# Storing from ScalarE's queue what ScalarE has made, with the planner's ranks found anew

## The chip, the core and the metric

The kernel runs on one core of one Trainium2 chip. A core has five engines that run side by side, each with its own instruction stream that is worked off in order: TensorE (PE; its weight loads are shown as PEld), VectorE (DVE), ScalarE (ACT), GpSimd (POOL) and SyncE (SP). They wait for each other through semaphores. DMAs are started from the instruction stream of an engine: SyncE, ScalarE and GpSimd start them here. An instruction at the head of a stream that waits holds all that stand behind it.

The metric is the device time of one execution in microseconds (us). Before the change it is 1215.32 us, the median of three runs (1213.84 to 1217.02).

## What is computed

Two transformer layers on 4096 tokens (16 sequences of 256) of width 128, all in float32, each sublayer followed by a residual sum and a layer norm:

```
x = layernorm(x + attention0(x))    # RMS norm, 16 heads of 64, softmax over 256 keys, output projection, bias
x = layernorm(x + moe0(x))          # 8 experts of hidden 256, top 2, gelu, biases, and one shared expert
x = layernorm(x + attention1(x))    # 16 heads of 8; each token attends over its own 16 heads
x = layernorm(x + moe1(x))          # 8 experts of hidden 512, top 2, gelu
```

The experts' weights of one token are its two largest softmax probabilities, not normalised anew. The layer-1 attention works inside a token: its scores are a 16 x 16 matrix for every token.

## The kernel before

**Tiles.** The tokens are cut into eight groups (0 to 7) of 512, each held in SBUF as a tile of 128 partitions x 4 chunks x 128. Group 7 is special: its second half is not routed by lists but goes through all experts with resident weights (the "dense" way, function `dense`, tiles ph_d, po_d, h_d, wd).

**Stages.** Layer-0 attention runs through all groups as 128 units, one pair of heads and one sequence each (`attention0`): projections (pq, pk, pv), scores (s), row maximum on VectorE (nm), exp on ScalarE and scaling on GpSimd (pr), transposes (t, copied to pT), values (po, copied to oT), and the output projection (py). When the groups of a wave are through, its mixture of experts starts while attention goes on with later groups. There are five waves in layer 0 and three in layer 1. A wave goes through:

- routing (`route`): top 2 of 8, and the position of each (token, expert) row in a list that is sorted by expert and padded to tiles of 128 rows. One small product (pc) counts across partitions.
- sending (`send`, L904 and L905): GpSimd writes the tokens' rows to their positions in DRAM (rows) with indirect DMAs.
- the lists (`lists`): in blocks of up to four tiles, SyncE loads the rows (xq, L1014) and the expert's weights (wa, L1035 or L1039; wb, L1048; the expert's number is read into a register at L997). TensorE transposes the rows (px, copied to xqT), does the first product (ph, L1098), ScalarE the gelu (h, L1071 or L1077), TensorE the second product (po_e, L1118). Function `stored` copies po_e to a tile yq, on VectorE or ScalarE, and SyncE stores yq to DRAM (outs, L1136). There are 46 such stores. yq has three buffers.
- gathering (`gathered`, L934 and L948): GpSimd reads each token's two rows back from outs (y), and VectorE adds them with their gates.
- a layer norm (`normed`). In layer 0 the layer-1 attention follows (`attention1`, `chunk1`: pqkv, copied to qkv; then products and reduces qk_prod, sc, av_prod and o, mostly on VectorE and GpSimd). In layer 1, `last` norms into a tile ye (one buffer) and stores it to the output (L1431); the dense half does the same at the end of `sequence` (L1595). These are nine output stores.

`normed` scales either on VectorE (L399) or, with two more small GpSimd instructions, on ScalarE (L409). ScalarE has to load a table (ACT_TABLE_LOAD) whenever it goes from exp to gelu or back.

**What sets the order.** The order of every engine's stream is settled when the program is built, by a planner written into the kernel. Each piece of work is a strand (a Python generator). A strand says when it could go on and on which engine. The planner keeps an estimated clock per engine (`clk`), advances it by `work(engine, us, ...)`, and always takes the strand with the smallest start less a lead. Lead and rank come from the table `KEYS` (one pair of rank and lead for each kind of work), and from `PACE` for the sixteen halves of attention. Further constants steer choices: `COPY` (VectorE or ScalarE for a copy, in `copied`), `FAVOUR` (GpSimd or VectorE for a product), `SWITCH` and `SWITCH_BACK` (when to change ScalarE's table), and `SUMS` (from what lead of TensorE over VectorE the sums of the layer-1 attention go to TensorE, as the products o_sums, L1274). `moved` is the estimate of a DMA: the issuing engine's time, then a shared pipe. No instruction is moved after this.

Of the kernel before, what the change touches and what calls it, by code (L numbers as in the profile page):

```python
# [28 lines left out]
LAST = NG - 1  # L29
# [8 lines left out]
def two_layers(  # L38
# [98 lines left out]
    def cleared(layer, w):  # L137
# [13 lines left out]
        "copy qk": (-0.126, 0.098),  # L151
        "copy v": (0.258, 0.464),
        "copy p": (0.365, 0.67),
        "copy o": (-2, 0.171),
        "softmax": (-0.332, 0.347),
        "softmax 2": (-0.557, 0.071),
        "summed": (-1.741, 0.444),
        "normalised": (0.126, 0.737),
        "heads": (-0.897, 0.036),
        "w route": (0.203, 0.017),  # L160
        "w send": (-0.299, 0.32),
        "w shared": (-0.925, 0.219),
        "w loads": (-0.335, 0.546),
        "w turns 0": (-0.74, 0.23),
        "w turns 1": (-0.883, 0.07),
        "w firsts 0": (-0.387, 0.019),
        "w firsts 1": (1.618, 0.545),
        "w gelu": (-0.526, 0.095),
        "w seconds 0": (-0.551, 0.301),
        "w seconds 1": (1.137, -0.645),  # L170
        "w stored": (-1.046, -0.735),
        "w gathered 0": (0.929, 0.295),
        "w gathered 1": (0.397, -0.379),
        "w qkv": (-1.874, 0.602),
        "w attention1": (0.552, 0.037),
        "w attention1 2": (0.862, 0.362),
        "w sums": (0.545, 0.099),
        "w normed": (-0.751, 0.178),
        "d loads": (-1.222, 0.561),
        "d route": (0.341, 0.516),  # L180
        "d firsts": (-0.612, -0.163),
        "d gelu": (0.532, 0.418),
        "d seconds": (-0.409, -0.744),
        "d added": (-0.448, 0.337),
        "d normed": (-0.4, 1.013),
    }
    PACE = [-1.37, 1.462, -1.273, -1.636, 1.503, -0.385, -0.54, 1.281]
    PACE += [1.979, 0.872, 0.936, -0.178, 0.47, 1.169, 0.679, 1.086]
    now = [0]
    COPY = -0.06  # L190
    SUMS = 7.789
    FAVOUR = 0.378
    SWITCH, SWITCH_BACK = 0.582, 1.515
# [44 lines left out]
    def moved(size, *after, us=0.45, row=2048):  # L238

        at = max(work("SP", us, *after) + 0.1, pipe[0])  # L240
        pipe[0] = at + size / (270e3 if row >= 1024 else 200e3)
        return max(pipe[0], at + size / 150e3) + 1.6
# [6 lines left out]
    def closed(place, at):  # L249
        ends[place[0]][place[1]] = at  # L250
        return at
# [132 lines left out]
    def normed(y, o, tag, at):  # L384
# [12 lines left out]
        if max(clk["DVE"], at) + 1.9 <= max(clk["ACT"], at) + 1.4:  # L397
            for c in range(n):
                nc.vector.tensor_scalar(  # L399
                    o[:, c, :], y[:, c, :], mv[:, c, 0:1], r[:, c : c + 1], ALU.subtract, ALU.mult  # L400
                )
            return work("DVE", 0.05 + 0.35 * n, at, ports=True)
# [7 lines left out]
        return work("ACT", 0.35 * n, at)  # L410
# [558 lines left out]
    def lists(r):  # L969
# [159 lines left out]
        def stored(i, place, po, at):  # L1129
# [3 lines left out]
            y, k = Y.tile([P, QT, D], "yq")  # L1133
            at = closed(place, copied(y[:, 0:n, :], po[:, 0:n, :], at, free))
            yield at, "SP"
            nc.sync.dma_start(  # L1136
# [3 lines left out]
            Y.done[k] = r.stored[i] = moved(n * 65536, at, row=512)  # L1140
# [282 lines left out]
    def last(r, part):  # L1423
# [4 lines left out]
        at = yield from normed(tokens(part), y, "n1", at)  # L1428
        yield at, "SP"
        b = c0 // 2  # L1430
        nc.sync.dma_start(  # L1431
# [3 lines left out]
        return work("SP", 0.6, at)  # L1435
# [133 lines left out]
    def sequence(b=1):  # L1569
# [23 lines left out]
        at = yield from normed(x, y, "n1", at)  # L1593
        yield at, "SP"
        nc.sync.dma_start(out=grouped(out, LAST)[:, b], in_=y.rearrange("p c d -> p (c d)"))  # L1595
        held.remove("y1")
        work("SP", 0.6, at)
# [66 lines left out]
```

## Time and profile before

The profile is of one execution, which is not one of the three timed ones.

| quantity | value |
|---|---|
| median of the runs | 1215.32 us |
| profiled execution: its own time | 1245.39 us |
| profiled execution: span of its instructions | 1243.7 us |
| mean granted clock of TensorE in it | 0.943 of full |
| PE busy | 1109.0 us (89%) |
| DVE busy | 900.2 us (72%) |
| ACT busy | 706.0 us (57%) |
| POOL busy | 705.7 us (57%) |
| DMA moved | 132.47 MB, mean 107 GB/s |

The page has a row of digits for each engine: the span in 40 equal slices, each digit the busy share in tenths; PEclk is the clock that the throttle granted TensorE, also in tenths. The chain of waits follows the last instruction back, at each step to what released it, and gives start, length and what ran; "issue" is time in which an engine waited for nothing that the profile shows. Lists of waits give the engine and line, what it waited for, the total in us, the number of waits and the longest. SPq is SyncE's queue, which issues DMAs.

The rows of the stores, from the answers on the tiles yq and ye (duration least, median, most in ns; first and last start in us):

```profile
L1136 SPq DMA_DIRECT2D outs<-yq x46: 359/448/1400, 211.4 to 1211.8; - x46
L272 ACT COPY yq<-po_e x36: 478/585/672, 206.8 to 1205.3; 128x512 f32<-128x512 f32 x32, 128x384 f32<-128x384 f32 x4
L270 DVE COPY yq<-po_e x10: 548/686/693, 201.6 to 1211.2; 128x512 f32<-128x512 f32 x6, 128x384 f32<-128x384 f32 x4
L1431 SPq DMA_DIRECT2D out_dram<-ye x8: 345/383/1532, 1166.5 to 1240.5; - x8
```

### The profile page before, as it was taken

What the parts mean: (1) busy time and instruction counts of PE and PEld (TensorE: products, weight loads), DVE (VectorE), ACT (ScalarE), POOL (GpSimd) and SP (SyncE); (2) the same over time, 40 slices, a digit from 0 to 9 for tenths busy, and PEclk for the clock granted to TensorE, in tenths of its full rate; (3) what the DMA queues carried; (4) which work ended last, traced back from release to release, by engine and by line L of the source; (5) the groups of instructions that cost most, each with busy time, mean ns of one, the idle gap of its engine ahead of it and who ended that gap; (6) DMA issues with size and microseconds to landing.
All of it is one profiled execution on the core that took longest, in us unless ns stands there. A gap on an engine that the chain in (4) does not pass through costs nothing.

```text
span 1243.7 us, 22712 instructions
## 1 busy us (share of the span) xinstructions
PE 1109.0 (89%) x7336; PEld 814.5 (65%) x7336; DVE 900.2 (72%) x1811; ACT 706.0 (57%) x2050; POOL 705.7 (57%) x1089
## 2 busy tenths in 40 slices
PE   9999999979999999999998899987838896797883
PEld 5566667665665666766655677655738795697883
DVE  5767675478878888754877998888878795793433
ACT  5556566476665667676674687653544552342432
POOL 4434372557555468524769557767873546446666
PEclk9999999989999999999999999987888897798997
DMA  8900023430000021151003240135458874684952
GB/s 260 270 1 1 1 86 111 132 106 14 1 5 1 1 63 58 35 145 45 18 4 100 80 133 21 29 119 164 144 162 232 257 230 129 197 245 125 288 177 70
DMA packets 187208, 132.47 MB, mean 107 GB/s; under 512 B 12745, under 2 KB 171474, under 8 KB 187090
## 3 DMA queue, kind: packets, MB, share of 16 engines
q1 hardware_dynamic: 179410, 115.27, 31.6%
q0 software_dynamic: 7680, 15.74, 4.1%
q8 instruction: 59, 0.97, 0.3%
q14 instruction: 59, 0.48, 0.1%
HBM read 97.94 MB, written 33.03 MB: 105 GB/s over the span
## 4 chain that ended last, share of the span: by engine, by line
PE 66%; DVE 11%; POOL 8%; issue 6%; ACT 4%; DMA 2%; SPq 1%; ACTq 0%; DVEq 0%; POOLq 0%
PE s L574 9%; PE po L612 9%; PE t L591 9%; PE po_e L1118 6%; PE ph L1098 6%; POOL rows L905 5%; PE py L629 4%; PE pv L528 4%; PE pq L510 4%; PE pk L510 3%; DVE qk_prod L1216 2%; DMA xq<-rows 2%; PE po_d L1541 1%; POOL pr L558 1%; DVE sc L1220 1%
## 5 line engine op out<-in xcount | busy, mean ns | idle before, releaser
L558 POOL TENSOR_SCALAR pr<-pr,rs 128x256 f32<-128x256 f32 x512 | 253.0, 511 | 220.6 <-DVE rs L554 136.7
L543 ACT ACTIVATE pr<-s,nm 128x256 f32<-128x256 f32 x512 | 235.5, 474 | 26.1 <-DVE nm L537 23.0
L537 DVE TENSOR_REDUCE nm<-s 128x4 f32<-128x1024 f32 x128 | 156.1, 1220 | 58.0 <-PE s L574 53.2
L905 POOL DMA_INDIRECT rows<-x,r_pi x120 | 130.7, 1089 | 58.6 <-DVE r_pi L853 24.4
L934 POOL DMA_INDIRECT y<-outs,r_pi x120 | 120.0, 1000 | 65.8 <-issue 27.4
L612 PE MATMUL po<-pT,v 128*64 128x256 f32 x1024 | 146.0, 397 | 7.2 <-ACT h L1077 3.1
L1098 PE MATMUL ph<-xqT,wa 128*128 128x128 f32 x1028 | 132.8, 287 | 16.6 <-issue 14.2
L591 PE MATMUL t<-ident,pr 128*128 128x128 f32 x1024 | 144.4, 283 | 0.8 <-ACT h L1077 0.8
L591 PEld LDWEIGHTS t<-ident,pr 128*128 128x128 f32 x1024 | 115.7, 145 | 42.4 <-POOL pr L558 20.6
L1098 PEld LDWEIGHTS ph<-xqT,wa 128*128 128x128 f32 x1028 | 126.9, 202 | 22.6 <-issue 16.8
L270 DVE COPY pT<-t 128x512 f32<-128x512 f32 x163 | 106.8, 686 | 42.2 <-PE t L591 38.3
L574 PEld LDWEIGHTS s<-kT,qT 64*128 64x128 f32 x896 | 77.1, 186 | 84.2 <-issue 73.1
L574 PE MATMUL s<-kT,qT 64*128 64x256 f32 x896 | 127.0, 402 | 0.0
L1292 POOL TENSOR_TENSOR av_prod<-sc,qkv 128x1024 f32<-128x1024 f32 x35 | 89.9, 2577 | 50.7 <-ACT sc L1254 35.3
L272 ACT COPY oT<-po 128x256 f32<-128x256 f32 x99 | 36.9, 373 | 130.6 <-PE po L612 119.6
L612 PEld LDWEIGHTS po<-pT,v 128*64 128x64 f32 x1024 | 65.1, 137 | 67.6 <-issue 18.9
L543 ACT ACTIVATION_READ_ACCUMULATOR pr<-s,nm 128x1 f32 x512 | 105.5, 206 | 0.0
L1118 PE MATMUL po_e<-wb,h 128*128 128x128 f32 x648 | 84.3, 292 | 5.5 <-issue 5.5
L1118 PEld LDWEIGHTS po_e<-wb,h 128*128 128x128 f32 x648 | 82.6, 209 | 5.3 <-issue 4.8
L1216 DVE TENSOR_TENSOR qk_prod<-qkv 128x1024 f32<-128x1024 f32 x64 | 82.8, 1294 | 1.8 <-ACT qkv L272 1.8
L1267 DVE TENSOR_REDUCE o<-av_prod 128x64 f32<-128x1024 f32 x62 | 73.3, 1200 | 11.3 <-POOL apart L904 9.7
L1220 DVE TENSOR_REDUCE sc<-qk_prod 128x128 f32<-128x1024 f32 x64 | 78.1, 1220 | 2.2
(233 smaller groups left out, 1971.0 us busy)
## 6 DMA issues: line engine op xcount, KB each, us to landing
wa<-in_w_dram SPq DMA_DIRECT2D x190, 128.0 KB
wa<-in_w_dram SPq DMA_DIRECT2D x81, 256.0 KB
wb<-in_w_dram SPq DMA_DIRECT2D x81, 256.0 KB
xq<-rows SPq DMA_DIRECT2D x38, 256.0 KB
outs<-yq SPq DMA_DIRECT2D x38, 256.0 KB
rows<-clear SPq DMA_DIRECT2D x3, 1472.0 KB
rows<-clear SPq DMA_DIRECT2D x1, 2496.0 KB
rows<-clear SPq DMA_DIRECT2D x2, 1216.0 KB
```

The source lines that it names most:

```text
L270: nc.vector.tensor_copy(o, i)
L537: nc.vector.tensor_reduce(nm[u], s, AX.X, ALU.max, negate=True)
L543: nc.scalar.activation(pr[u][:, i, :], s[:, i, :], AF.Exp, bias=nm[u][:, i : i + 1], accum_out=su[u][:, i : i + 1],)
L558: nc.gpsimd.tensor_scalar(pr[u][:, i, :], pr[u][:, i, :], rs[:, i : i + 1], 1.0, ALU.mult, ALU.mult)
L574: nc.tensor.matmul(sc[u][:, j, qc, :], q[part, ts(qc, P)], k[part, :], start=True, stop=True,)
L591: nc.tensor.transpose(t[:, kc, ts(qc, P)], pr[u][:, 2 * j + qc, ts(kc, P)], ident)
L612: nc.tensor.matmul(po[j * DH : (j + 1) * DH, :], vs[g, p // 4, 2 * b + kc][:, ts(h, DH)], pT[u][j][:, kc, :], start=(kc == 0), stop=(kc == 1),
L905: i = nc.gpsimd.indirect_dma_start(out=rows[layer][w][:, :], out_offset=bass.IndirectOffsetOnAxis(ap=r.pos[:, k, c : c + 1], axis=0), in_= ...
L934: nc.gpsimd.indirect_dma_start(out=y, out_offset=None, in_=outs[layer][w][:, :], in_offset=bass.IndirectOffsetOnAxis(ap=r.pos[:, k, c0 + c ...
L1098: nc.tensor.matmul(ph[:, q - q0, c, :], was[i, q][0][:, c, :], xTs[i][0][:, q, :], start=True, stop=True)
L1118: nc.tensor.matmul(po[:, q, :], hs[i, q][0][:, c, :], wbs[i, q][0][:, c, :], start=(c == 0), stop=(c == nh - 1))
L1216: nc.vector.tensor_tensor(m, q3[:, ts(j, HALF)].unsqueeze(2).to_broadcast(full), k3.unsqueeze(1).to_broadcast(full), ALU.mult)
```

## The change

Two things are changed together.

First, a store goes out from the engine that made the tile. `normed` can now say which engine did the scaling (`who=True`). In `stored`, `last` and at the end of `sequence`, the DMA is issued by ScalarE if ScalarE wrote the tile, directly behind the copy or the scaling in ScalarE's own stream. If VectorE wrote it, the store stays with SyncE and its strand still has to be chosen by the planner for SyncE. `moved` charges the issue to that engine, and the estimate of a list store's issue is 0.55 us in place of 0.45.

Second, all constants of the planner but FAVOUR are new: the ranks and leads in KEYS, PACE, COPY, SUMS, SWITCH and SWITCH_BACK. The planner's rules are as before. With other constants the order of the instructions differs nearly everywhere on all engines, and so do some choices of engine.

```diff
     KEYS = {
-        "copy qk": (-0.126, 0.098),
-        "copy v": (0.258, 0.464),
-        "copy p": (0.365, 0.67),
+        "copy qk": (-0.686, 0.094),
+        "copy v": (0.244, 0.271),
+        "copy p": (-0.684, 0.892),
...
-    COPY = -0.06
-    SUMS = 7.789
+    COPY = -0.04
+    SUMS = 6.956
     FAVOUR = 0.378
-    SWITCH, SWITCH_BACK = 0.582, 1.515
+    SWITCH, SWITCH_BACK = 0.754, 1.251
...
-    def moved(size, *after, us=0.45, row=2048):
+    def moved(size, *after, us=0.45, row=2048, e="SP"):
 
-        at = max(work("SP", us, *after) + 0.1, pipe[0])
+        at = max(work(e, us, *after) + 0.1, pipe[0])
...
-    def normed(y, o, tag, at):
+    def normed(y, o, tag, at, who=False):
...
-            return work("DVE", 0.05 + 0.35 * n, at, ports=True)
+            at = work("DVE", 0.05 + 0.35 * n, at, ports=True)
+            return (at, "DVE") if who else at
...
-        return work("ACT", 0.35 * n, at)
+        at = work("ACT", 0.35 * n, at)
+        return (at, "ACT") if who else at
...
+            was = clk["ACT"]
             at = closed(place, copied(y[:, 0:n, :], po[:, 0:n, :], at, free))
-            yield at, "SP"
-            nc.sync.dma_start(
+            by = "SP" if clk["ACT"] == was else "ACT"
+            if by == "SP":
+                yield at, "SP"
+            (nc.sync if by == "SP" else nc.scalar).dma_start(
                 out=outs[layer][w][t0 * P : (t0 + n) * P, :].rearrange("(t p) d -> p t d", p=P),
                 in_=y[:, 0:n, :],
             )
-            Y.done[k] = r.stored[i] = moved(n * 65536, at, row=512)
+            Y.done[k] = r.stored[i] = moved(n * 65536, at, us=0.55, row=512, e=by)
...
-        at = yield from normed(tokens(part), y, "n1", at)
-        yield at, "SP"
+        at, by = yield from normed(tokens(part), y, "n1", at, who=True)
+        if by == "DVE":
+            yield at, "SP"
         b = c0 // 2
-        nc.sync.dma_start(
+        (nc.scalar if by == "ACT" else nc.sync).dma_start(
             out=grouped(out, g)[:, b : b + n // 2], in_=y.rearrange("p (b c) d -> p b (c d)", b=n // 2)
         )
         held.remove("y1")
-        return work("SP", 0.6, at)
+        return work("SP" if by == "DVE" else "ACT", 0.6, at)
```

The end of `sequence` is changed in the same way as `last`. In the changed program 37 of the 46 list stores and 7 of the 9 output stores are ScalarE's.

More of the change, by code (lines that the diff above doesn't have):

```diff
@@ L150, in two_layers @@
     KEYS = {
-        "copy qk": (-0.126, 0.098),
-        "copy v": (0.258, 0.464),
-        "copy p": (0.365, 0.67),
[L154 to L185, printed above, removed]
-    }
-    PACE = [-1.37, 1.462, -1.273, -1.636, 1.503, -0.385, -0.54, 1.281]
-    PACE += [1.979, 0.872, 0.936, -0.178, 0.47, 1.169, 0.679, 1.086]
+        "copy qk": (-0.686, 0.094),
+        "copy v": (0.244, 0.271),
@@ new lines, in two_layers @@
+        "copy p": (-0.684, 0.892),
+        "copy o": (-1.278, 0.176),
+        "softmax": (-1.102, 0.352),
+        "softmax 2": (-1.24, 0.071),
+        "summed": (-1.561, 0.534),
+        "normalised": (0.213, 0.857),
+        "heads": (0.758, 0.041),
+        "w route": (-0.095, 0.009),
+        "w send": (-0.805, 0.292),
+        "w shared": (-1.313, 0.682),
+        "w loads": (0.692, -0.26),
+        "w turns 0": (-1.62, 0.042),
+        "w turns 1": (0.65, 0.1),
+        "w firsts 0": (-0.064, 0.058),
@@ new lines, in two_layers @@
+        "w firsts 1": (-1.063, 0.177),
+        "w gelu": (-1.14, 0.085),
+        "w seconds 0": (-0.593, 0.301),
+        "w seconds 1": (-0.568, -0.8),
+        "w stored": (0.539, -0.771),
+        "w gathered 0": (1.071, 0.312),
+        "w gathered 1": (0.161, 0.063),
+        "w qkv": (-0.627, 0.578),
+        "w attention1": (0.941, 0.114),
+        "w attention1 2": (1.532, 0.369),
+        "w sums": (0.284, 0.089),
+        "w normed": (0.63, 0.178),
+        "d loads": (0.236, 1.5),
@@ L189, in two_layers @@
+        "d route": (-0.056, 0.858),
+        "d firsts": (-1.413, -0.167),
+        "d gelu": (-0.132, 0.623),
+        "d seconds": (-0.286, -0.8),
+        "d added": (-0.324, 0.509),
+        "d normed": (0.282, 0.357),
+    }
+    PACE = [-1.351, 0.954, -1.992, -2, 0.862, -0.568, -0.54, 1.22]
+    PACE += [1.308, 1.716, 1.027, -1.705, 0.282, 1.453, 0.585, 1.633]
     now = [0]
-    COPY = -0.06
-    SUMS = 7.789
+    COPY = -0.04
+    SUMS = 6.956
     FAVOUR = 0.378
-    SWITCH, SWITCH_BACK = 0.582, 1.515
+    SWITCH, SWITCH_BACK = 0.754, 1.251
@@ L1592, in sequence @@
         y = sb.tile([P, 2, D], FP, tag="y1", name="ye", bufs=1)
-        at = yield from normed(x, y, "n1", at)
-        yield at, "SP"
-        nc.sync.dma_start(out=grouped(out, LAST)[:, b], in_=y.rearrange("p c d -> p (c d)"))
+        at, by = yield from normed(x, y, "n1", at, who=True)
+        if by == "DVE":
+            yield at, "SP"
+        (nc.scalar if by == "ACT" else nc.sync).dma_start(
+            out=grouped(out, LAST)[:, b], in_=y.rearrange("p c d -> p (c d)")
+        )
         held.remove("y1")
-        work("SP", 0.6, at)
+        work("SP" if by == "DVE" else "ACT", 0.6, at)
     begin(normalised(0), key("normalised"))
```

## The prediction

> **What bounds the kernel now.** First the page's slices, then the table of stretches, then the chain of waits, then SyncE's own waits.
>
> ```profile
> PE   9999999979999999999998899987838896797883
> ACT  5556566476665667676674687653544552342432
> PEclk9999999989999999999999999987888897798997
> ```
>
> In 24 of the first 27 slices (31 us each) TensorE is busy to 90% or more, at nearly its full clock. After that it has holes, and its granted clock drops with them. The stretches put sizes on this (columns: stretch, length, then busy time of PE, weight loads, DVE, ACT, POOL with counts, granted clock, DMA share, GB/s):
>
> ```profile
> 0.00:840.00 840.00, 805.57 (x5172) 534.82 (x5172) 631.40 (x1203) 538.37 (x1726) 469.32 (x790) 0.98 0.23 68
> 840.00:1120.00 280.00, 214.80 (x1514) 196.12 (x1513) 223.50 (x421) 125.05 (x244) 157.84 (x195) 0.85 0.65 195
> 1120.00:1224.00 104.00, 88.59 (x655) 83.60 (x653) 39.15 (x162) 39.15 (x73) 68.98 (x90) 0.93 0.64 185
> ```
>
> Until 840 us TensorE is 96% busy: whatever is rearranged there can win 840 - 805.6 = 34 us at most. From 840 to 1120 VectorE is the busiest (80%) and TensorE stands for 65 us and runs at 0.85 of its clock. From 1120 to 1224 no engine is full but TensorE, and the last 20 us are gathers, norms and the final stores. So time moves in the tail from 840 on. The longest links of the chain there:
>
> ```profile
> 1030.02 10.88 issue
> ...
> 1067.69 7.09 PE o_sums L1274 x32
> ...
> 1078.02 3.55 PE o_sums L1274 x32
> ...
> 1124.71 13.03 issue
> 1137.74 0.37 SPq L1136
> ```
>
> The last pair is the change's own subject: SyncE's queue stood for 13.03 us with the store of L1136 at its head until the copy into yq was made, and everything behind it stood too. Over the whole run:
>
> ```profile
> SPq L1136 <- ACT yq L272: 82.7, 10, 13.4
> ```
>
> That is ten waits of a store for ScalarE's copy, 82.7 us in total, the longest 13.4 us.
>
> **1. Stores on ScalarE's queue.** The listing of the built kernel puts 37 of the 46 list stores and 7 of the 9 output stores on ScalarE; 9 and 2 stay on SyncE because VectorE made them. The Trainium skill (DMA: Bandwidth & Descriptors, Issuing engines are not separate DMA queues) speaks against any gain: DMAs of all queues run on the same 16 DMA engines, and starting them from more engines saves only the sequencer's time to issue. By that rule the change saves 44 x 0.448 us (the store's median in its row) = 19.7 us of an engine that bounds nothing: 0. By the row it removes waiting in order, which the rule doesn't count. I follow the row, place by place:
> - 1124 to 1138: behind the store wait nine weight loads and the xq reads of the last list, whose first read is issued at 1152.46. With SyncE free they could go as soon as GpSimd's sends are down. The last send runs 1139.3 to 1140.3; the nearest landing of a small DMA in the chain took 2.44 us; so 1142.7, and 9.7 us is the most to be had. TensorE was not idle meanwhile (16.04 of 20 us in 1140 to 1160, other work), so I take **-5** (0 to -9.7). Late next: those sends.
> - The four waits of 12.4 to 13.4 us at 220, 260, 560 and 740 us lie where TensorE is nearly full. Reads of xq held TensorE 4.4 us at 205 to 285 and 1.0 us at 545 to 600, and nothing of the kind at 725 to 760: **-2** (0 to -5.4). Attention's matmuls hide the rest.
> - About 1040 (7.7 and 6.8 us): here the store was late because ScalarE was stuck 18.0 us with a copy into qkv at its head. The copy moves with the store; **0**.
>
> What it costs: 44 issues on ScalarE, 19.7 us, of which 31 (13.9 us) come after the last softmax. ScalarE is 45% busy in 840 to 1120, so most are covered. Cover fails where a gelu or a PSUM-freeing copy is queued behind: TensorE waits for that. **+1.5** (0 to +8).
>
> What it adds as a wait: each plain DMA, on either queue, takes one of eight completion counters in turn, and waits until the DMA eight before it has landed. On SyncE that held up SyncE alone. Now a store at ScalarE's head holds exps, gelus and copies behind it, and TensorE behind those. No row of before shows it. From below: 0, if the eighth DMA before has always landed. From above: the chain's reads of xq landed in 3.5 to 4.7 us; if SyncE ran a full landing late for the 24 tail stores, half reaching TensorE, 24 x 3 x 0.5 = +36. A block of four tiles makes about ten DMAs and takes TensorE twice 3.57 us, and in the listing the eighth before is mostly a weight load put nearly one block earlier; so it normally has more than 4.7 us. I am near the lower end: **+1**. In return SyncE may run seven DMAs past an unfinished store; that is in the gains above.
>
> **2. Ranks found anew.** This reorders nearly everything, so I count what the listing holds in the tail, by row durations.
> - No score or value sum goes to TensorE any more. The two o_sums links, 10.6 us of the chain, go. Two VectorE reduces of 1.200 us come instead: -8.2 if nothing else is late. But VectorE is the fullest engine there, and px and py between the links wait for their own data; I take half, **-4** (0 to -8.2).
> - VectorE work between the last attention row maximum and the last routing's positions: 242 us before, 238 after, by rows (two qk_prod and two sc reduces of 1.2 us moved ahead, five sc subtractions of 0.54 us to GpSimd, against two o reduces and some scalings). VectorE sets this stretch: **-3** (0 to -4). Late next: GpSimd, which takes these subtractions.
> - Behind the last routing's count (pc) TensorE has 8 more ph and 16 more po_e instructions. The chain gives 3.57 us for 32 records, two to an instruction, so 0.223 us each: 24 x 0.223 = 5.4 us. TensorE has 15 us of holes there: **+3** (0 to +5.4).
> - Table loads go from 46 to 58, eight of the twelve after the last softmax. The Trainium skill (ScalarE: Activation LUTs, Terms) gives about 2.7 us for a load; by that, 12 x 2.7 = 32 us. The row decides:
>
> ```profile
> L1254 ACT ACT_TABLE_LOAD x12 | 15.4, 1283 | 0.2
> ```
>
> So 12 x 1.283 = 15.4 us, 10.3 of it in the tail. They stand before an exp or gelu that someone waits for, but ScalarE holds only 4% of the chain: **+1.5** (0 to +10.3).
> - Copies shifted in attention: 27 more 128x512 copies on VectorE (27 x 0.69 = 18.5 us), 13 fewer of 128x256, and the reverse on ScalarE. TensorE is full there and both engines below 77%: 0 (-3 to +3).
>
> The last stores gain a queue hop of under 0.1 us: 0. PE, the loads, the sends, the gathers are the same in number.
>
> **Sum.** -5 - 2 + 1.5 + 1 - 4 - 3 + 3 + 1.5 = **-7**. Made against the profiled span of 1243.7 us (1245.39 with what lies around it) that is 1236.7. The profiled run is 30 us over the median of the runs, at a mean granted clock of 0.943, so I carry over the difference and not the level: 1215.32 - 7 = **1208**.
>
> **Rivals.**
> - *A new blockage in order, slower.* Before has two that the plan did not mean: ScalarE 18.0 us behind one qkv copy, TensorE 15.2 us behind one t_x that waits for VectorE's o. An order changed in nearly every row can meet a third: a transpose or copy put too early, with ready work behind it. Price 15 to 18 us, place 840 to 1120, on top of -7: about 1224. It decides from 11 us of new standing on. For: the order was not tried against these traces' delays, such as a VectorE multiply of 1.13 us that takes 5.70 beside GpSimd. Against: the same reshuffle may dissolve the two old ones (10.9 us of chain at 1030), giving 1197.
> - *ScalarE held by its stores, slower.* The eight-back wait above, in the stretch where DMA is at 0.64 to 0.90 of its share. If each of the 31 tail stores holds ScalarE 1.3 us (issue apart) and half reaches TensorE, that is +20: 1228. It decides from 0.7 us a store. For: late loads on SyncE stay common, it waits 95.4 us for po_e alone. Against: ScalarE is 45% busy there.
> - *Hidden anyway, no change.* The sends on GpSimd and VectorE's chain set the tail whoever issues the stores, and orders cancel: 1215.
>
> That the change doesn't do what it says is excluded by the listing.
>
> **How the numbers follow.** Forecast 0.43, new blockage 0.26, ScalarE held 0.20, no change 0.11. A measurement of this kernel can tell about 0.3% (3.6 us) from no change. So faster 0.43, within 0.3% 0.11, slower 0.46. The forecast is the likeliest single case; its own range is 1195 to 1211. With the rivals the range is 1193 to 1234.
>
> **What would show it.** Right: no chain link of ten microseconds that ends at an outs store on SyncE's queue; no o_sums; the first xq read of the last list within 3 us of the last send; ScalarE's wait for DMAs under 10 us in all. The blockage: a wait of 10 us or more at TensorE or ScalarE between 840 and 1120 for a tile of the layer-1 attention, and more throttled slices there. ScalarE held: outs rows on ScalarE's queue preceded by microseconds of waiting for a DMA, gelus late, TensorE idle behind h. I am wrong at the root if attention, 0 to 840, moves by over 10 us.

## The result, and the profile after

The changed kernel takes 1228.82 us (median of four runs, 1227.25 to 1234.38), the kernel before on the same chip 1215.74 us. The ratio is 1.0117, with a 95% interval of 1.009 to 1.0143: the change costs 13.1 us. The forecast was 1208 us, so its sign is wrong. The range, 1193 to 1234, holds the time.

Two things have to be known to read the numbers below. Every batch of runs was made on one chip together with the kernel before, and that same kernel took 1215.7, 1213.5, 1249.2, 1243.5, 1248.9 and 1245.2 us in the six batches. So a time is compared only inside its batch. And the profile from which the prediction was made (span 1243.7 us) belongs to the higher of these levels, while the times that it was set beside belong to the lower.

Lines in the changed kernel stand 2 to 7 below those of before: the list stores are L1141 (before L1136), the layer-1 exponential L1259 (L1254), the copies L270 and L272 as before. The page of the profile after (span 1226.7 us), the same slices as were shown of before:

```profile
PE   9999999979999998999999899898666799678795
ACT  5555576475776662776566577565454366463442
PEclk9999999999999997999999989899787899788797
```

In the sixteenth slice (460 to 491 us), in the middle of attention, TensorE is at 8 and its clock at 7 tenths. Before had 9 and 9 there. The stretches of the changed kernel:

```profile
0.00:840.00 840.00, 802.23 (x5105) 531.50 (x5106) 632.36 (x1177) 528.64 (x1695) 464.70 (x776) 0.97 0.22 65
840.00:1120.00 280.00, 217.23 (x1534) 195.23 (x1532) 238.12 (x474) 140.89 (x273) 181.10 (x225) 0.87 0.69 207
1120.00:1224.00 104.00, 81.75 (x638) 78.28 (x636) 39.17 (x167) 43.26 (x82) 69.61 (x89) 0.89 0.65 191
```

Until 840 us TensorE is as busy as before, but only 5105 of its records are done where before had 5172 (5180 in the second profile of before, at the level of this one). Busy time alone hides this: at half a clock TensorE is busy for longer with the same work (a pair of 128x512 products took 2.08 us at clock 0.50 and 1.02 us at 1.00). From 840 to 1120 it is as full as before (217 us against 215 in the first and 221 in the second profile of before).

What the change was to do, it did. The stores, from the tile yq, and SyncE's own waits:

```profile
L1141 ACTq DMA_DIRECT2D outs<-yq x37: 366/366/440, 200.4 to 1180.9; - x37
```

```profile
SPq L1141 <- DVE yq L270: 123.8, 4, 87.3
```

The waits of a store for ScalarE's copy (82.7 us) are gone. What is left are four waits for VectorE's copies, 123.8 us; before had three of them, 9.2 us in all. So stores hold SyncE's queue no less than before, but in other places: the longest wait, 87.3 us, lies between 262 and 350 us, where TensorE was busy for 86.2 of 88 us. The chain has no o_sums any more.

### The profile page after: what moved, and what is told of

It reads as the page before. It is cut to its first block, busy times and chain, and to the rows that moved or that the text cites. A ratio compares the mean times of both kernels' runs of the same rounds, so it can differ in the third digit from the quotient of the medians.

```text
span 1226.7 us, 22445 instructions
## 1 busy us (share of the span) xinstructions
PE 1101.2 (90%) x7272; PEld 805.0 (66%) x7272; DVE 909.7 (74%) x1816; ACT 712.8 (58%) x2049; POOL 715.4 (58%) x1089
## 4 chain that ended last, share of the span: by engine, by line
PE 62%; DVE 16%; POOL 11%; issue 4%; ACT 4%; DMA 2%; SPq 0%; ACTq 0%; DVEq 0%; POOLq 0%
PE s L576 10%; PE po L614 9%; PE t L593 9%; POOL rows L907 5%; PE pv L530 4%; PE ph L1100 4%; PE pq L512 4%; PE po_e L1120 4%; PE pk L512 3%; PE py L631 3%; DVE qk_prod L1221 2%; DVE o L1272 2%; DVE sc L1225 2%; DVE av_prod L1297 2%; DMA y<-outs,r_pi 2%
## 5 line engine op out<-in xcount | busy, mean ns | idle before, releaser
L560 POOL TENSOR_SCALAR pr<-pr,rs 128x256 f32<-128x256 f32 x512 | 246.7, 500 | 211.6 <-DVE rs L556 145.3
L936 POOL DMA_INDIRECT y<-outs,r_pi x120 | 118.3, 986 | 45.9 <-issue 24.9
L270 DVE COPY pT<-t 128x512 f32<-128x512 f32 x176 | 114.6, 686 | 40.6 <-PE t L593 40.2
L1100 PE MATMUL ph<-xqT,wa 128*128 128x128 f32 x1028 | 127.7, 283 | 15.4 <-DVE xqT L270 5.2
L593 PEld LDWEIGHTS t<-ident,pr 128*128 128x128 f32 x1024 | 112.3, 142 | 43.7 <-POOL pr L560 23.8
L1100 PEld LDWEIGHTS ph<-xqT,wa 128*128 128x128 f32 x1028 | 123.3, 198 | 18.3 <-DVE xqT L270 5.6
L1297 POOL TENSOR_TENSOR av_prod<-sc,qkv 128x1024 f32<-128x1024 f32 x42 | 107.0, 2560 | 38.5 <-ACT sc L1259 32.4
L272 ACT COPY oT<-po 128x256 f32<-128x256 f32 x112 | 41.7, 372 | 142.4 <-PE po L614 142.4
L1221 DVE TENSOR_TENSOR qk_prod<-qkv 128x1024 f32<-128x1024 f32 x64 | 86.3, 1349 | 0.6 <-ACT qkv L272 0.6
L950 DVE SCALAR_TENSOR_TENSOR x<-y,r_gate,x 128x128 f32<-128x128 f32 x120 | 47.5, 401 | 50.3 <-DMA y<-outs,r_pi 48.6
L1120 PE MATMUL po_e<-wb,h 128*128 128x128 f32 x648 | 79.0, 282 | 0.0
```

Source lines behind the costliest of these rows:

```text
L270: nc.vector.tensor_copy(o, i)
L560: nc.gpsimd.tensor_scalar(pr[u][:, i, :], pr[u][:, i, :], rs[:, i : i + 1], 1.0, ALU.mult, ALU.mult)
L593: nc.tensor.transpose(t[:, kc, ts(qc, P)], pr[u][:, 2 * j + qc, ts(kc, P)], ident)
L936: nc.gpsimd.indirect_dma_start(out=y, out_offset=None, in_=outs[layer][w][:, :], in_offset=bass.IndirectOffsetOnAxis(ap=r.pos[:, k, c0 + c ...
L1100: nc.tensor.matmul(ph[:, q - q0, c, :], was[i, q][0][:, c, :], xTs[i][0][:, q, :], start=True, stop=True)
L1120: nc.tensor.matmul(po[:, q, :], hs[i, q][0][:, c, :], wbs[i, q][0][:, c, :], start=(c == 0), stop=(c == nh - 1))
```

## The experiments

Theories. **O**: the new order costs the 13 us, the queue nothing. **S**: the stores on ScalarE cost them. **P**: the profiled execution of before was not like the timed ones, and gains read from it do not exist in them. Later **B** and **D** say where the order loses.

### The kernel before, profiled again

The kernel is unchanged.

> The kernel before, unchanged, for a second profile. The first profile's span was 28 us above the median of the runs. Theory P (the profiled execution was an unusual one): span near 1214 us, and the two longest links of its tail, 10.9 us at 1030 and 13.0 us at 1125, are gone or under 4 us each. Rival (they belong to the kernel, and profiling costs 28 us): span again near 1243 us with both links.

It took 1214.1 us, span 1212.4. The chain of waits of this execution, its longest links from 1030 to 1130 us:

```profile
1038.37 4.38 DVE av_prod L1292
...
1053.66 7.09 PE o_sums L1274 x32
...
1125.69 6.79 DMA xq<-rows
```

The link of 13.03 us from which the prediction took its -5 is not there, nor is the one of 10.88 us, although the stores' waits are (SyncE's list still shows 75.0 us in 13 waits for ScalarE's copy). The first read of the last list's rows is issued at 1125.69, 3.5 us behind the last send (1121.26 to 1122.23). In the first profile that gap was 12.2 us. P holds for these two links: at the level of the timed runs there was next to nothing to free at SyncE. It doesn't hold for the o_sums, which stand in the chain here too (7.09 and 3.56 us).

### Queue and order taken apart

First the order of before on every engine, with the 44 stores moved to ScalarE directly behind its copy:

```diff
+            by = nc.sync if clk["ACT"] == was else nc.scalar
+            if by is nc.scalar:
+                by.dma_start(out=to, in_=y[:, 0:n, :])
             yield at, "SP"
...
+            if by is nc.sync:
+                by.dma_start(out=to, in_=y[:, 0:n, :])
```

> The order of before on every engine; only the 36 list stores and 8 output stores whose tile ScalarE made leave from ScalarE's queue, right behind the copy. Theory O (the new order costs the 13 us, the queue nothing): within 4 us of before. Theory S (stores on ScalarE cost it): 8 to 15 us slower than before, ScalarE waiting several us in all for earlier DMAs. The gain my prediction had counted (a store no longer holds SyncE): 5 to 8 us faster.

1215.77 us against 1213.46, ratio 1.0014 (1.0004 to 1.0025). On before's order the queue is worth nothing; it costs 2 us. ScalarE waited there for a DMA twice behind its first load, 2.5 us before a gelu and 2.3 us before a ye.

Then the changed kernel's order with all stores on SyncE, at the same places of the program:

```diff
-            (nc.sync if by == "SP" else nc.scalar).dma_start(
+            nc.sync.dma_start(
```

> The order of after on every engine; all stores issued by SyncE, at the place in its stream where the plan had ScalarE issue them. Theory O: as slow as after, near 1228 us. Theory S: back to 1214 to 1218 us. If a store at the head of SyncE's queue costs what I predicted: slower than after by 5 to 10 us.

1240.67 us against 1213.46, ratio 1.0205 (1.0182 to 1.0229). This is more than the changed kernel loses, so on the new order ScalarE's queue wins something. That compares two batches; in the sixth batch both stood side by side:

> The changed kernel unaltered, as the measure for the run that follows on the same chip: 1.010 to 1.022 of before, by the three chips so far.

> The order of the changed kernel on every engine, with all stores issued by SyncE at the same places of the program. If ScalarE's queue is worth something on this order, as the first such run suggests (some 10 us, all of it behind 1000 us): 0.5 to 1.2% slower than the changed kernel on this chip, so that queue and order work against each other and the order costs more than the whole loss. Rival: within 0.3% of the changed kernel; the queue is worth nothing here either, as on before's order, and the order alone makes the whole difference.

1267.42 us for the changed kernel (1.0161 of before, 1.0126 to 1.0196) and 1283.13 us with SyncE's stores (1.0288, 1.025 to 1.0326): the queue is worth 15.7 us on this order, give or take some 6 by the two intervals. In the trace with SyncE's stores its list of waits shows again what the change removes:

```profile
SPq L1141 <- ACT yq L272: 97.1, 22, 13.8
```

By their copies into yq the two kernels are within 4.2 us of each other until 950 us and some 6 us apart up to 1167 us; then the copies of the last list come 18 to 24 us later. S is refuted. The order costs 27 us in one batch (1240.7 - 1213.5) and 38 us in the other (1283.1 - 1245.2), and the queue gives 11 to 16 of it back, the 11 being a comparison across batches (1.0205 against 1.0117).

### The constants alone, and the stores alone, planned anew

The constants of the change in before's code, and the changed code with before's constants; both times the planner lays everything anew.

> The code of before (all stores on SyncE, planned there) with the new constants, planned anew. Theory O: 8 to 18 us slower than before, like after. Theory S: within 4 us of before. The plan differs from both, so a single plan's luck of some 10 us is in it.

> The changed code with the planner's constants of before: the planner lays the order anew with 41 stores on ScalarE's queue. Theory O (constants fit one plan; any new plan drawn with them loses tens of us whatever the queue does): 1230 to 1330 us, with TensorE's granted clock under 0.94. Rival (the stores alone are what the change is worth, and the new constants cost it): 1205 to 1216 us, near the run of before's order with the stores on ScalarE (1215.8 us).

1321.9 us (1.0884, 1.0851 to 1.0917) and 1334.27 us (1.0671, 1.0623 to 1.0719). The first lies far above the 8 to 18 us that were expected. So a set of constants belongs to one planner. Neither half of the change can be had by planning anew, and the size of the change's own effect cannot be read from such runs. For that, orders have to be kept, as above and below.

### Where the order loses: one exponential

The traces of before (the second one) and after agree within 1 us from unit 64 to unit 72 of attention (435 us, by the start of the row maximum nm). The last unit comes at 822.0 us in before and 842.1 us in after. The stretch table from 460 to 520 us, first before and then after:

```profile
460.00:520.00 60.00, 60.00 (x383) 40.10 (x382) 49.50 (x78) 42.99 (x135) 45.54 (x67) 1.00 0.13 41
```

```profile
460.00:520.00 60.00, 52.33 (x296) 37.80 (x295) 41.91 (x60) 30.30 (x86) 29.31 (x40) 0.83 0.28 84
```

Before runs TensorE without a break at full clock. After loses 7.7 us of idleness, and 52.3 x 0.17 = 8.9 us by the clock: some 16.6 us. VectorE, ScalarE and GpSimd do less in the same time too. The timeline of after shows what stood (start, length, engine, line, operation; in brackets the idle time before it and what ended it):

```profile
473.71 0.42 ACT L1259 ACTIVATE sc<-sc 128x256 f32<-128x256 f32 x1 [8.16 <-DVE sc L1250]
474.03 0.56 ACT L272 COPY wT<-pw 9x512 f32<-9x512 f32 x1
...
474.64 2.08 PE L1179 MATMUL ph<-xT,w 128*128 128x512 f32 x2 [6.04 <-ACT wT L272]
```

ScalarE's next instruction is the exponential of one layer-1 chunk, and it waits 8.16 us for VectorE's subtraction. Behind it stands the copy of wT, which has long been ready (its product pw started at 466.11) and which frees the PSUM bank that TensorE's next product ph needs. TensorE stops for 6.04 us. Its granted clock follows (stretches of 2 us, the clock is the third number from the end):

```profile
470.00:472.00 2.00, 0.00 (x0) 0.00 (x0) 1.96 (x3) 0.00 (x0) 1.96 (x3) 1.00 0.11 37
472.00:474.00 2.00, 0.00 (x0) 0.00 (x0) 1.93 (x4) 0.29 (x1) 1.84 (x5) 0.83 0.00 0
474.00:476.00 2.00, 1.36 (x2) 0.50 (x2) 1.97 (x3) 1.97 (x4) 1.97 (x2) 0.50 0.10 33
...
488.00:490.00 2.00, 2.00 (x10) 1.25 (x10) 1.73 (x4) 0.59 (x1) 0.10 (x1) 0.50 0.00 0
490.00:492.00 2.00, 2.00 (x17) 1.46 (x14) 0.66 (x2) 0.85 (x2) 0.52 (x1) 0.90 0.00 0
```

TensorE works again from 474.6 us on, and its clock is at half until 490.4.

Theory B took this exponential for the cause. It was put behind what it held, together with the VectorE and ScalarE steps that follow from it; TensorE's and GpSimd's orders stay, and ScalarE loads its table twice more (60 loads for 58). Then the same was done at a second place, at 699 us. ScalarE's order at the first:

```diff
 ACTIVATE pr<-s,nm
-ACTIVATE sc<-sc
 COPY wT<-pw
 ACTIVATE h<-ph,b
 ACTIVATE h<-ph,b
+ACTIVATE sc<-sc
```

> The kernel after with one step put elsewhere: the exponential of one layer-1 attention chunk (the one that ScalarE started at 473.71 us after 8.16 us of waiting) stands behind the copy of wT and the two gelus of the shared expert that had stood behind it, with the steps that read it; every other instruction keeps its place and its engine, and ScalarE's table is loaded twice more. Theory B (one ScalarE instruction that waits for VectorE holds the copy that frees TensorE's bank; TensorE stops for 6 us and its clock is then halved for 16): the stop of 6.04 us is gone, the granted clock is 1.0 from 470 to 490, attention unit 80 comes at 476 to 500 us and not at 524, and the time falls to 1213 to 1222 us, 0.998 to 1.006 of before. Rival A (absorbed: attention has slack behind the place, as the fall of the lag from 48 to 14 us by unit 104 suggests): unit 80 comes early, the last unit comes within 4 us of its 842 us all the same, and the time is 1225 to 1232 us. Rival C (the clock falls for another reason than the stop): the stop is gone, the clock is at 0.5 to 0.7 somewhere in 470 to 500 us all the same, and unit 80 stays over 510 us.

> As the run before it, and the same done at the second place: the exponential that ScalarE started at 698.93 us after waiting 6.36 us stands behind the copies of kT and v, the two gelus and the copy of oT. Theory B: TensorE's stop of 3.2 us and the clock of 0.60 at 700 to 710 us are gone too, and the time is 2 to 6 us under that of the run with one place mended. Rival A: the two runs agree within 0.2%. If both places together bring the last attention unit from 842 to 822 to 828 us and the end does not follow by at least half of it, then the tail behind attention, and not attention, carries the 13 us.

1262.52 us and 1260.14 us against 1249.18, ratios 1.0092 (1.0057 to 1.0127) and 1.0079 (1.0051 to 1.0108). Unit 80 still comes at 526.7 us and 523.4 us (523.9 in after and 475.7 in before, in the profiles of the lower level). From 460 to 520 us TensorE is now busy for 50.72 us at clock 0.89 with one place mended and 49.34 us at 0.89 with both: the one stop is gone and others stand around it. Theory B as written failed. The exponential alone is not the cause of the whole loss. Whether moving it won a part is open, since the changed kernel did not run beside these two: against its first batch (1.0117) they win nothing outside the intervals, against its three batches at the level of this one (1.0147, 1.0219 and 1.0161, below) some 7 to 17 us.

### A place that the change did not touch

In before (second profile) TensorE stops 4.28 us until 658.92 us, because a memset of ones stands behind a row of scatters on GpSimd. It was given to VectorE, and with it the five like it at the other waves and in the dense half.

```diff
-            nc.gpsimd.memset(r.w[:, :, NE:NE0], 1.0)
+            nc.vector.memset(r.w[:, :, NE:NE0], 1.0)
```

> The kernel before with one engine exchanged: the memset that puts the ones for the shared expert into the list weights is VectorE's and not GpSimd's, where it stood behind a row of indirect scatters at 658.74 us and TensorE waited 4.28 us for it with the clock at 0.84 and 0.82 around it. Theory B in a place that the change did not touch: TensorE no longer stops there, the clock is 1.0 from 650 to 670 us, and the units from 104 on come 4 to 8 us earlier; if attention carries the end, the time falls to 1205 to 1211 us, 0.993 to 0.998 of before. Rival A (absorbed behind the place): the same time as before within 0.2%.

1251.59 us against 1249.18, ratio 1.0017 (0.9996 to 1.0038). The stretch tables, first before (its first profile, at the level of this batch) and then this run, show why nothing came of it:

```profile
650.00:660.00 10.00, 7.43 (x46) 3.80 (x44) 9.61 (x18) 4.27 (x12) 7.92 (x11) 1.00 0.31 97
680.00:690.00 10.00, 6.25 (x34) 3.56 (x33) 8.86 (x8) 7.87 (x17) 8.51 (x6) 0.93 0.21 66
```

```profile
650.00:660.00 10.00, 8.86 (x55) 4.92 (x53) 9.59 (x19) 4.09 (x9) 8.06 (x13) 1.00 0.22 70
680.00:690.00 10.00, 4.08 (x24) 2.48 (x21) 7.67 (x7) 6.71 (x15) 9.27 (x7) 0.86 0.23 72
```

TensorE's busy time from 650 to 660 rose from 7.43 to 8.86 us, and from 680 to 690 it fell from 6.25 to 4.08. The stop before pw is 2.93 us and not 4.28 (it now waits for VectorE's memset), and one that stood at 688 us grew from 3.75 to 5.92 us. What was won was lost again 30 us later.

### Does TensorE's time in attention reach the end?

The two findings suggested that attention has slack. So 120 transposes of nothing were put into before's order, once in attention (at 455 us in the trace) and once behind it (from 912 us on):

```diff
+            if clk["PE"] > 470 and not spent:
+                spent.append(1)
+                idle_bank = ps_m.tile([P, GT], FP, tag="m", name="t_spent")
+                for c in range(120):
+                    nc.tensor.transpose(idle_bank[:, ts(c % NC, P)], ident, ident)
```

> The kernel before with 120 transposes of nothing, some 15.6 us of TensorE's time, put into its order where the attention stands at about 470 us; nothing else moves. It asks whether time that TensorE loses in attention reaches the end. Theory B (attention carries): the last attention unit comes 13 to 17 us later and the end 11 to 16 us later, 1.009 to 1.013 of before. Rival A (absorbed behind attention, because the lists' loads and VectorE set the pace there): the last unit is late, the end by less than 4 us, under 1.0033.

> The same 120 transposes put at about 900 us, among the lists behind attention. Theory B: TensorE is no more the bound there than in attention, 5 to 16 us at the end. Rival A's other half (the tail is where the time is set): 11 to 16 us, 1.009 to 1.013. If the lists behind attention wait for their loads and not for TensorE, less than 5 us, under 1.004.

1263.65 us against 1243.47, ratio 1.013 (1.0076 to 1.0185), and 1258.66 us, ratio 1.0121 (1.0058 to 1.0183). That is 9 to 23 us and 7 to 23 us, for transposes that took 13.3 and 15.2 us of TensorE's time in the traces. The intervals are wide, but "absorbed" (under 1.0033) lies outside both. What TensorE loses in attention is late at the end.

### Where the order loses: two chunks of layer-1 attention

With its new ranks the planner starts the seventh and eighth chunk of layer-1 attention earlier: their maxima c_mx stand at 472.8 and 489.4 us in after, at 491.1 and 501.8 us in before. Theory D says that their VectorE and GpSimd work, some 20 us, stands in the way of the copies and maxima that attention waits for. First the chunks' steps were put later, one behind every second step of other work, from about 485 us on and then from about 500:

> The changed kernel unaltered, on the chip of the three runs that follow, since chips differ by up to 3% for the same kernel (before took 1213.5 us on one and 1249.2 us on another). Theory O (the new order costs it): 1.009 to 1.015 of before here too. Rival (the loss belongs to the chip of the first measurement): under 1.006.

> The kernel after with the steps of two layer-1 attention chunks put later within the stretch from 460 to 525 us, one behind every second step of the other work; TensorE's and GpSimd's order is the same. Theory D (VectorE's steps of layer-1 attention stand ahead of the copies and maxima for which TensorE's attention waits; what ended last at 470 us was VectorE's chain and not the one exponential, so that moving the exponential alone changed nothing): TensorE has done as much by 520 us as before had, which it misses by some 11 us of work in after; unit 80 comes by 510 us and not at 524; the last unit 5 to 15 us earlier than in after, and the time 5 to 13 us under after's. Rival A (absorbed): TensorE's work at 520 us recovers, the time stays within 0.3% of after's. Rival E (no order of these chunks helps, VectorE has too much to do there): nothing recovers.

> The kernel after with the same steps of the same two layer-1 chunks put later still, from about 500 us on instead of 485, one behind every second step. Theory D with room: VectorE is under 60% busy from 510 to 560 us in after, so there TensorE need not wait for it; the stop at 470 us is gone as in the run that moved them less far, no new one over 3 us comes behind it, and the time is 5 to 15 us under after's. Rival E (the stop moves again): within 0.4% of after.

In the batch of the first two the changed kernel took 1262.94 us (1.0147, 1.0101 to 1.0194) and the run with the chunks later 1264.07 us (1.0158, 1.0113 to 1.0203). Still later gave 1264.36 us against 1267.42 for the changed kernel. The timeline of the first shows the stop in a new place:

```profile
502.75 2.57 PE L759 MATMUL po<-pT,v 128*64 128x256 f32 x8 [3.71 <-DVE pT L270]
...
512.20 2.27 PE L738 MATMUL t<-ident,pr 128*128 128x128 f32 x8 [6.88 <-POOL pr L705]
```

The stop at 470 us is gone, and TensorE waits before 502.75 us for a copy that stands behind the chunks' steps on VectorE, and before 512.20 us for GpSimd's scaling, which waits 6.20 us for a reciprocal behind the chunks' head sums on VectorE. Rival E of these expectations holds for every place that was tried.

So the work itself was taken away at its place. For these two chunks the products, sums and head sums were left out in both kernels; memsets of the small results stand for them:

```diff
-            nc.vector.tensor_tensor(m, q3..., k3..., ALU.mult)
-            nc.vector.tensor_reduce(sc1[:, ts(j, HALF)], m, AX.X, ALU.add)
+            nc.vector.memset(sc1[:, ts(j, HALF)], 0.0)
...
-            (nc.gpsimd if e == "POOL" else nc.vector).tensor_tensor(m, sc1..., v3..., ALU.mult)
...
-            nc.vector.tensor_reduce(o[:, c, ts(j, P // 2)], m..., AX.X, ALU.add)
+            nc.vector.memset(o[:, c, ts(j, P // 2)], 0.0)
```

> The kernel after with work left out: for the seventh and eighth chunk of layer-1 attention the products of q and k, their sums, the products with v and the head sums are not computed (four small memsets each stand in their place), some 16 us of VectorE and 4.7 us of GpSimd that stand between 460 and 512 us; all else keeps its place. Theory D (the two chunks stand in VectorE's and GpSimd's way where attention needs them, and no finer order of them helps): TensorE's stop at 468 to 475 us and the halved clock behind it are gone, TensorE has done as much by 520 us as in before, the last attention unit comes 10 to 20 us earlier and the time falls 8 to 16 us under after's, to 0.998 to 1.006 of before. Rival A (the lag at 520 us is not what the end is late by): less than 4 us.

> The kernel before with the same work of the same two chunks left out. There it stands between 475 and 525 us and TensorE does not stop beside it, with its clock at 1.0. Theory D: hidden work, 0 to 4 us under before. Rival F (VectorE is the bound of attention in both, wherever its work stands): 8 to 16 us under before, as in after.

> The changed kernel unaltered on the same chip as these two, as the measure for the first of them. By the earlier runs 1.009 to 1.015 of before; Theory O expects it again.

| kernel, same batch | us | to before |
|---|---|---|
| before | 1248.92 | 1 |
| before, two chunks left out | 1250.29 | 1.0010 (0.9994 to 1.0027) |
| after | 1275.22 | 1.0219 (1.0193 to 1.0246) |
| after, two chunks left out | 1255.39 | 1.0055 (1.0032 to 1.0078) |

The same work taken out of before is worth nothing, and taken out of after 19.8 us, three quarters of what after loses there and more than the 8 to 16 us expected. Rival F is refuted: the work is hidden where before has it. The work is taken from VectorE and from GpSimd at once, so these runs don't tell which of the two matters. Nor do they say where the rest of what the order costs is lost. The stretch tables from 460 to 520 us, first before with the chunks left out, then after, then after with them left out:

```profile
460.00:520.00 60.00, 60.00 (x383) 39.59 (x382) 35.22 (x74) 41.50 (x127) 35.56 (x68) 1.00 0.17 50
```

```profile
460.00:520.00 60.00, 46.17 (x230) 29.04 (x228) 42.78 (x48) 21.94 (x59) 25.87 (x31) 0.74 0.25 73
```

```profile
460.00:520.00 60.00, 54.85 (x354) 38.91 (x353) 28.30 (x63) 34.35 (x95) 24.16 (x41) 0.94 0.37 110
```

The last attention unit comes at 857.7 us in after and at 835.6 us without the chunks, and of these 22 us 18 are left at the last copy into yq and at the end. The stop in this execution of after was longer than in the first, and its timeline shows one reason:

```profile
479.76 5.69 DVE L1250 TENSOR_TENSOR sc<-sc,c_mx 128x256 f32<-128x256 f32 x1
480.53 4.62 POOL L1297 TENSOR_TENSOR av_prod<-sc,qkv 128x1024 f32<-128x1024 f32 x2
...
485.48 0.42 ACT L1259 ACTIVATE sc<-sc 128x256 f32<-128x256 f32 x1 [17.59 <-DVE sc L1250]
485.81 0.56 ACT L272 COPY wT<-pw 9x512 f32<-9x512 f32 x1
...
486.42 2.07 PE L1179 MATMUL ph<-xT,w 128*128 128x512 f32 x2 [10.14 <-ACT wT L272]
```

VectorE's subtraction, 0.42 us otherwise, took 5.69 us beside two GpSimd products of the chunk before, and the exponential waited 17.59 us. This is the smaller part: the subtraction also began 6.5 us later than in the first execution. VectorE had stood for 5.18 us before its copy into oT at 470.30, 2.7 us of it with the product ready (at 467.59), while GpSimd alone was at work with its scatters. Why it stood is open.

For the changed kernel, its versions with the stores on ScalarE, and before without the chunks, the loss in this one stretch goes with the loss at the end. The first number is 60 us less TensorE's busy time, plus the busy time times what the clock lacks; it is rough, since the clock is a mean over the stretch and the trace is one execution:

| kernel | lost from 460 to 520 us | late at the end (median, own batch) |
|---|---|---|
| before, two chunks left out | 0 | 1.4 |
| after, two chunks left out | 5.2 + 3.3 = 8.4 | 6.5 |
| after, exponential moved | 9.3 + 5.6 = 14.9 | 13.3 |
| after, two exponentials moved | 10.7 + 5.4 = 16.1 | 11.0 |
| after, first batch | 7.7 + 8.9 = 16.6 | 13.1 |
| after, fourth batch | 13.8 + 6.5 = 20.3 | 19.5 |
| after, chunks later | 13.5 + 7.9 = 21.4 | 20.6 |
| after, chunks still later | 15.4 + 7.6 = 23.0 | 19.2 |
| after, sixth batch | 11.9 + 11.6 = 23.4 | 22.2 |
| after, fifth batch | 13.8 + 12.0 = 25.8 | 26.3 |

The trace is not always near the median: the execution of the fourth batch that lost 20.3 us here was only 8.9 us late at the end. With all stores on SyncE the order loses much the same here (16.6 and 24.9 us), but the end is 27.2 and 37.9 us late; the 11 and 13 us between are near what the queue is worth.

The chunks were left out at the higher level only. That the same work makes the 13 us of the first batch is read from its trace, not tested.

No version came out that beats both kernels. The nearest to before is before itself with its stores on ScalarE.

## Why the prediction was wrong

**The step that failed is the one that costed the order in attention at nothing**: "Copies shifted in attention: [...] TensorE is full there and both engines below 77%: 0 (-3 to +3)". From 460 to 520 us alone it lost some 16.6 us in the execution shown, and 20 to 26 us in the other three executions of the same kernel. The item counts copies alone. What moved and cost was the work of two layer-1 chunks, 18 and 12 us earlier than in before; taking it out of the new order won 19.8 us. The reason given was a mean over 840 us, and it asked what could be won there (34 us at most), not what could be lost. In those 60 us the order that VectorE and ScalarE follow, not their share of busy time, decides whether TensorE is fed. The prediction named its own test: "wrong at the root if attention, 0 to 840, moves by over 10 us". The last unit moved by 20 (by 16 against the profile that the prediction used, where it comes at 826.2 us).

**The rival "a new blockage in order" came nearest, in the wrong place.** It said a transpose or copy put too early with ready work behind it, 15 to 18 us, about 1224 us in all, between 840 and 1120. In the trace it is an exponential put too early with a ready copy behind it, at 465 to 474 us. But moving that exponential did not bring the time back (1.0092 and 1.0079); leaving out the chunks' products and sums, behind which it waits, came nearest (1.0055, beside 1.0219 in the same batch). That the rival's total is near the measured one is in part luck: it is the order's 27 to 38 us less what the queue gave back, and the rival had neither. I looked for it where TensorE had holes already. It was made where TensorE had none.

**-5 for SyncE at 1124, and -4 for o_sums.** The -5 was read from a link of one execution at another level than the times. In the second profile of before the gap behind the last send is 3.5 us and not 12.2, and with 2.44 us for a send to land, as the prediction took it, at most 1 us could be won. In after it is 10.3 us (last send until 1127.07, first read at 1137.40), because weight loads stand ahead of it in SyncE's list; the sign named in the prediction, within 3 us, did not come. "Carry over the difference and not the level" was the wrong rule: a difference made of links that only one level shows does not carry over. The o_sums are in the chain at both levels and went from it as predicted; what that is worth alone was not tried.

**-2 for the four early waits, 0 for 1040, +1.5 for the issues, +1 for the eight-back wait.** Together with the -5 this is the queue, -4.5 in the sum. Measured on before's order +2.3 us (1.0014), on the new order -15.7. The prediction had no term for this: what a queue is worth depends on the order that it serves. ScalarE's waits for a DMA in after are 1.5 us at its first load and 1.8 us before a ye, none before a list store, so the rival "ScalarE held by its stores" is refuted and the step's lower end was right. An issue on ScalarE took 0.366 us, not 0.448.

**-3 for VectorE's work, +3 for TensorE's 24 instructions, +1.5 for the table loads.** These were not tested one by one. The lag is 20 us at the last attention unit, 6 at the last positions (1111.5 against 1105.3) and 14 at the end: the stretch from 840 to the last routing does better than before, and the last one worse by 8 us. One piece of that last loss can be named from the trace (TensorE waits 9.30 us at 1142.30 for a transpose behind ScalarE's scaling of x), but what it is worth was not measured. The table load is 1.283 us again, as assumed. The count of slices at the start of the prediction is one too high (23 of the first 27 are at 90% or more), which changes nothing.

**"Hidden anyway"** is refuted by both signs: the queue alone and the order alone each move the time, by +2 to -16 and by +27 to +38 us. The orders didn't cancel; the queue hid part of what the order cost.

## What to carry to other kernels

A change of order is priced at the densest stretch and not at the emptiest: where the bounding engine has no hole, look for the instruction that waits at the head of another engine's stream with ready work behind it, and count the throttled clock after the stop as well. When mending one such wait does not bring the time back, the cause is wider; take away the work that feeds it, in both kernels, and see in which of them it matters. Run the unmended kernel beside every mended one. And set a profile beside times of its own level only.

## What the runs showed of the hardware

- **After a stop of TensorE its clock stayed at half for 3.7 us or for about 16.** After the stop of 6.04 us it came back at 490.4 us, 15.7 us after TensorE had begun again (474.64), and after the stop of 10.14 us in the fifth batch 16.0 us after (486.42 to 502.4; there it had been at half since 471.7 us, from a shorter stop). TensorE was busy throughout. In the fourth batch, at the same place and before the same products, the stop was 10.41 us and the clock came back 3.7 us after it (TensorE began again at 482.43):

```profile
484.00:486.00 2.00, 2.00 (x3) 0.50 (x2) 1.97 (x4) 1.06 (x2) 0.00 (x0) 0.50 0.00 0
486.00:488.00 2.00, 2.00 (x11) 1.34 (x11) 2.00 (x4) 0.59 (x1) 1.72 (x1) 0.98 0.00 0
```

  The Trainium skill (TensorE: Matmul & The Clock Gate, Part 1) expects full clock after some 3.4 us of sustained work. The third stop agrees and the first two do not. By that rule the 6 us stop would have cost under 2 us more, an estimate (half of 3.4 us); here it cost about 8 (half of 15.7 us), more than the stop itself. Why it took so long was not tried.
- **A VectorE subtraction with both inputs in SBUF took 5.69 us beside GpSimd's products, and 0.42 us otherwise**; in the run with one exponential moved, a product of q and k took 6.17 instead of 1.22 us beside two of them. The Trainium skill (SBUF — State Buffer, Who interferes with whom) says that such an instruction contends with a GpSimd instruction that reads SBUF, and the loser blocks wholly. The trace agrees that one of them blocks. Why it was VectorE the rows don't tell: the subtraction's begins at 479.76 us, 0.77 us before that of GpSimd's first product, and GpSimd's two took 4.62 us together, no longer than two of the median, 2.348 us, take.
- **The same kernel took 1213 to 1216 us in two batches and 1243 to 1249 us in four.** The level does not go with the chip's number: the second batch (1213.5 us) and the sixth (1245.2 us) both ran on the chip numbered 0. By the copies into yq, the profiles of before at the two levels are within 7 us of each other until 1018 us and 32 us apart at the last copy. What slows the lists at the end on the one and not on the other stays open.
